# A two-layer graph transformer on one core: where the second layer's weight sums are kept at the border, and how many attention steps its first block takes

## The chip, the core and the metric

The kernel runs on one core of one Trainium2 chip. The metric is the time of one execution on the device in microseconds (us). Five engines work side by side: PE (TensorE: matmuls; PEld are its weight loads), DVE (VectorE), ACT (ScalarE), POOL (GpSimd) and SP (SyncE). Each runs its own instructions in order, and an instruction waits until what it needs has arrived. SP, ACT and POOL also issue the DMA transfers.

## The reference, cut to what matters

Two layers of the same form, with 2708 nodes, 512 features, 8 heads of 64 and a hidden width of 2048, all in float32. The adjacency is sparse, so a node attends to few others.

```python
def layer(h, adj, Wq, bq, Wk, bk, Wv, bv, Wo, bo, W1, b1, W2, b2, ln1_g, ln1_b, ln2_g, ln2_b):
    mask = adj.astype(float32) + eye(n)
    q, k, v = ((h @ W.T + b).reshape(n, 8, 64) for W, b in ((Wq, bq), (Wk, bk), (Wv, bv)))
    scores = einsum('nhd,mhd->hnm', q, k) / sqrt(64)
    attn = softmax(where(mask == 0, -1e9, scores))
    ctx = einsum('hnm,mhd->nhd', attn, v).reshape(n, 512)
    h1 = layer_norm(h + ctx @ Wo.T + bo, ln1_g, ln1_b)
    ff = relu(h1 @ W1.T + b1) @ W2.T + b2
    return layer_norm(h1 + ff, ln2_g, ln2_b)
x = layer(x, adj, *layer_0); x = layer(x, adj, *layer_1)
```

## The kernel before, in words

**Tiles and blocks.** The nodes are sorted by their number of neighbours and cut into 22 tiles of 128 (the last one, tile 21, has 20 rows). `CAPS` gives the longest list of neighbours in each tile. Two tiles make a block; a layer has 11 blocks, and the last is tiles 21 and 0. The code of `by_edges` issues everything in an order written out by hand.

**Attention** (`attend`, L1898 on) works on DVE, ACT and POOL. A step takes up to two neighbours per node: POOL gathers their keys and values (L1119, tile `kv`), DVE multiplies by the query (L1156) and sums per head (L1162), ACT takes the exponential (L1175) and weighs one neighbour's values (L1182), DVE weighs the other's (L1188) and adds (L1195). The weighing of a step is issued one step later. At a tile's end come a few small operations (L1203 to L1218) and the division on ACT (L1226), which gives `cx`. `loads` (L1249) issues the gathers three chunks ahead (`EARLY`). The `kv` tiles come from a ring of `KVB` = 5 places; in layer 1 `rows_of_keys` (L1233) adds the places of the weights `wk` and `wv`, which are free by then: seven in all, from its first gather on.

**Feed-forward** works on PE. A block has 16 chunks f of the hidden width: a product with W1 (tile `pf`), relu on ACT (`ft`), and a product with W2 into the accumulators `a0`, `a1`, three chunks later (`LAG`). In the blocks after `FORMED[n]` (1 in layer 0, 3 in layer 1), up to the last but one, `feed_forward_by_seven` (L1727) does the second product for pairs of chunks with seven matmuls in place of eight. It needs sums of the hidden values (L1735 to L1738, on DVE) and, for pairs 0 to 6, sums of blocks of W2, which are read back from `form_d` in HBM (L1720).

**How steps and blocks interleave.** At each chunk f of a block the loop calls `advance(x)`: x comes from tables (`PACES` for block 0, `PACE` for the blocks without the seven products, `PACE7` for those with them) and is added to a credit, which the next attention steps use up (a step of two neighbours costs 1, and no step starts with three `cx` waiting). At f = 10 and 11 `until` issues the steps that the next block's two tiles still need; then `attended` does the output projection, the residual and the first norm (its total is L1307). At the end of a block in layer 1 DVE takes the accumulators with another L1307; the rest of that norm follows in the next block (`ended`: squares on ACT, L1324; L1331 and L1333 on POOL; L1334 on DVE; scaling on ACT).

**The border of the layers.** In layer 0's last block (which has no seven products) SP loads layer 1's W1 and W2 as their places come free: pair j of W2 at f = 2j + 3. `form_apart` (L1677) makes layer 1's sums for pair j: four subtractions on DVE (L1684 to L1687) into the tile `forms`, and four stores of 128 KB to `form_d` (L1690). Pairs 0 to 4 are made at f = 7, 9, 11, 13 and 15 and stored from POOL's queue; pairs 5 and 6 follow the last keys and values and are stored from SP's. `staged` (L1669) takes three of the five `kv` places for `forms`; pair 6 uses the first of them a second time. `settle` (L1388) turns layer 1's short vectors at f = 13. When the block's chunks are done, DVE adds the accumulators of tile 21 to the residual (L1642, with three more additions at L636 since its 20 rows are summed in quarters, L1583), norms it (L1275 to L1290, L1281 on POOL), and PE transposes it (L1349) for layer 1's keys and values. Two queries of layer 1 from preloaded tiles (`zTs`) stand on PE around that transposition. Then `keys_values` finishes, its rows are put into `kv_d` (L1082), and layer 1 begins: some twenty queries on PE, with the first attention steps between them, and then its block 0.

**Use of the sums.** Layer 1 reads the fourth sum of each pair at block 3 (`form_in`, L1692), the other three from block 4 on.

Of the kernel before, what the change touches and what calls it, by code (L numbers as in the profile page):

```python
# [8 lines left out]
F32 = mybir.dt.float32  # L9
# [9 lines left out]
P = 128  # L19
DM = 512  # L20
# [3 lines left out]
NC = DM // P  # L24
# [13 lines left out]
SLOTS = 2  # L38
QB = 3
LAG = 3  # L40
KVB = 5
# [8 lines left out]
EARLY = 3  # L50
PACES = (
    (0.0,) * 4 + (0.85,) * 8 + (0.0,) * 2 + (0.8,) * 2,
    (0.75,) * 11 + (0.0,) * 2 + (0.9,) * 3,
)
PACE7 = (
    (0.0,) * 4 + (0.6,) + (1.3,) * 4 + (0.6,) * 2 + (0.0,) * 2 + (0.5, 0.8, 2.4),
# [431 lines left out]
def by_edges(ctx: ExitStack, tc: tile.TileContext, x, xT, adj, layers, out, redo):  # L488
# [9 lines left out]
    nc = tc.nc  # L498
# [16 lines left out]
    wts = ctx.enter_context(tc.tile_pool(name="wts", bufs=1))  # L515
# [4 lines left out]
    stage = ctx.enter_context(ExitStack())  # L520
# [15 lines left out]
    at = None  # L536
# [694 lines left out]
    places = []  # L1231
    written = [[] for _ in range(NL)]

    def rows_of_keys(n):

        if n == NL - 1 and not places:
            places.extend([None] * KVB + ["wk", "wv"])
        tag = places[0] if places else None
        if places:
            places.append(places.pop(0))  # L1240
        if tag is None:
            return at.tile([P, SLOTS, 2 * DM], F32, tag="kv", name="kv", bufs=KVB)
        kv = wts.tile([P, NC, DM], F32, tag=tag, name="kv")
        return kv.rearrange("p c n -> p (c n)").rearrange("p (s n) -> p s n", s=SLOTS)
# [113 lines left out]
    class Layer:  # L1358
        def __init__(self, n, w):
            self.n, self.w, self.w1, self.w2, self.due = n, w, [], [], None  # L1360
            self.apart, self.other = True, False
            self.stores = nc.sync

# [304 lines left out]

        def staged(self):  # L1669

            slots = []
            for _ in range(3):
                place = at.tile([P, SLOTS, 2 * DM], F32, tag="kv", name="forms", bufs=KVB)
                place = place.rearrange("p s n -> p (s n)")
                slots += [place[:, i * 2 * P : (i + 1) * 2 * P] for i in range(8)]
            return slots

        def form_apart(self, j, slots):
# [3 lines left out]
            i = 4 * j % len(slots)  # L1682
            t2, t3, t4, t1 = slots[i : i + 4]
            nc.vector.tensor_tensor(t3, b22, b12, ALU.subtract)  # L1684
# [333 lines left out]
    for n in range(NL):  # L2018
        last = n == NL - 1
        nxt = None if last else Layer(n + 1, layers[n + 1])  # L2020
        if n > 0:
            streamed = now.queries(order[10:16])
            got = {}
            ahead = attend(n, got)
            for _ in range(2):
                now.query(*pool.pop(0))
            next(ahead)
            both = now.two(order[8:10])
            pool += [(g, both[:, i]) for i, g in enumerate(order[8:10])]
# [36 lines left out]
        for k, block in enumerate(blocks):  # L2066
# [14 lines left out]
            for f, zs in enumerate(working):  # L2081
# [64 lines left out]
                if not last and not more:  # L2146
# [20 lines left out]
        if not last:  # L2167
# [69 lines left out]
```

## Time and profile before

| | us |
|---|---|
| median of 3 runs | 1830.86 (1828.04 to 1831.38) |
| the profiled execution's own time | 1829.8 |
| its span, first to last instruction | 1828.1 |
| PE busy | 1793.9 |
| DVE busy | 1463.7 |
| ACT busy | 1002.0 |
| POOL busy | 875.7 |

The stages of the span, from windows with PE's busy time in each: layer 0's keys, values and neighbour lists 0 to 150 (148.4), its queries 150 to 315 (163.2), its blocks to 1004 (682.1 of 689.0), its last block to 1064 (54.1 of 60.0), layer 1's queries to 1149.7 (85.4 of 85.7), its blocks 0 to 3 to 1409.8 (259.9 of 260.2), blocks 4 to 9 to 1782.3 (366.2 of 372.5), the last block and the end to 1828.1 (34.7 of 45.8).

How to read it: an engine is busy while it works on an instruction, and idle before one that waits; the trace names the instruction that ended the wait. The mean granted clock of PE is 0.994 of full speed.

### The profile page before, as it was taken

What the parts mean: (1) busy time and instruction counts of PE and PEld (TensorE: products, weight loads), DVE (VectorE), ACT (ScalarE), POOL (GpSimd) and SP (SyncE); (2) the same over time, 40 slices, a digit from 0 to 9 for tenths busy, and PEclk for the clock granted to TensorE, in tenths of its full rate; (3) what the DMA queues carried; (4) which work ended last, traced back from release to release, by engine and by line L of the source; (5) the groups of instructions that cost most, each with busy time, mean ns of one, the idle gap of its engine ahead of it and who ended that gap; (6) DMA issues with size and microseconds to landing.
All of it is one profiled execution on the core that took longest, in us unless ns stands there. A gap on an engine that the chain in (4) does not pass through costs nothing.

```text
span 1828.1 us, 23929 instructions
## 1 busy us (share of the span) xinstructions
PE 1793.9 (98%) x6839; PEld 1216.1 (67%) x6839; DVE 1463.7 (80%) x2599; ACT 1002.0 (55%) x3397; POOL 875.7 (48%) x847
## 2 busy tenths in 40 slices
PE   9999999999999999999999989999999999999987
PEld 4444455666777867778677534666666788788866
DVE  4986768987989889899895257968877899999943
ACT  5770435645556555564543204576766677677741
POOL 3334755534455544554430232546665765575412
PEclk9999999999999999999999999999999999999999
DMA  9997987756576676665652877946757887877621
GB/s 340 371 347 253 364 279 248 233 171 232 199 253 225 201 235 196 219 234 183 227 191 71 287 282 269 326 138 232 249 174 244 285 257 226 283 268 221 212 77 36
DMA packets 186296, 426.74 MB, mean 233 GB/s; under 512 B 20886, under 2 KB 83210, under 8 KB 186152
## 3 DMA queue, kind: packets, MB, share of 16 engines
q0 software_dynamic: 77520, 265.54, 43.8%
q1 hardware_dynamic: 98474, 137.96, 22.2%
q10 hardware_dynamic: 10158, 21.61, 3.1%
q8 instruction: 56, 0.92, 0.2%
q14 instruction: 88, 0.72, 0.1%
HBM read 357.13 MB, written 57.11 MB: 227 GB/s over the span
## 4 chain that ended last, share of the span: by engine, by line
PE 83%; DVE 8%; issue 4%; DMA 2%; ACT 2%; POOL 1%; POOLq 0%; DVEq 0%; SPq 0%; ACTq 0%
PE pf L1769 17%; PE c L1758 8%; PE k L626 8%; PE q L626 8%; PE v L626 8%; PE pf L1595 8%; PE o L626 7%; PE a L1568 7%; PE a L1758 6%; PE tp L1349 2%; DVE sc L1162 2%; DVE kv L1156 2%; PE a L1793 1%; PE a L1789 1%; DVE acc L1195 1%
## 5 line engine op out<-in xcount | busy, mean ns | idle before, releaser
L1119 POOL DMA_INDIRECT kv<-kv_d,listed x420 | 540.4, 1287 | 287.6 <-DVE acc L1195 129.8
L1769 PE MATMUL pf<-hT,w 128*128 128x256 f32 x1792 | 407.1, 379 | 1.6 <-ACT ft L1780 1.6
L1769 PEld LDWEIGHTS pf<-hT,w 128*128 128x128 f32 x1792 | 339.3, 190 | 58.3 <-issue 11.2
L1182 ACT ACTIVATE kv<-kv,p 128x64 f32<-128x64 f32 x1232 | 311.2, 336 | 5.0
L1156 DVE TENSOR_TENSOR kv<-kv,q 128x1024 f32<-128x1024 f32 (+1 forms) x222 | 257.1, 1158 | 11.2 <-DMA q<-q_d,ident_i 9.7
L1162 DVE TENSOR_REDUCE sc<-kv 128x16 f32<-128x1024 f32 (+1 forms) x222 | 258.0, 1162 | 7.6
L1195 DVE TENSOR_TENSOR acc<-acc,kv 128x1024 f32<-128x1024 f32 (+2 forms) x178 | 205.6, 1155 | 51.2 <-ACT kv L1182 37.3
L1595 PEld LDWEIGHTS pf<-hT,w 128*128 128x128 f32 x1024 | 178.4, 190 | 56.5 <-issue 33.5
L1595 PE MATMUL pf<-hT,w 128*128 128x256 f32 (+1 forms) x1024 | 214.7, 358 | 1.0 <-ACT ft L1606 0.9
L1780 ACT ACTIVATE ft<-pf,b 128x256 f32<-128x256 f32 x168 | 78.3, 468 | 214.7 <-PE pf L1769 212.1
L1568 PE MATMUL a<-w,ft 128*128 128x512 f32 x416 | 194.6, 592 | 0.0
L1175 ACT ACTIVATE p<-sc,listed 128x8 f32<-128x8 f32 x420 | 103.9, 296 | 129.6 <-DVE sc L1162 98.2
L1281 POOL TENSOR_TENSOR rd<-va,mhalf 128x1 f32<-128x1 f32 (+1 forms) x48 | 43.6, 908 | 234.6 <-DVE va L1279 234.5
L626 PE MATMUL o<-wo,cT 128*128 128x512 f32 x336 | 151.2, 594 | 2.3 <-issue 1.9
L1188 DVE TENSOR_TENSOR kv<-kv,p 128x512 f32<-128x512 f32 (+1 forms) x178 | 124.1, 697 | 6.3 <-ACT p L1175 6.1
L1568 PEld LDWEIGHTS a<-w,ft 128*128 128x128 f32 x416 | 77.7, 190 | 57.5 <-issue 52.3
L1331 POOL TENSOR_SCALAR va<-sq 128x1 f32<-128x1 f32 (+1 forms) x40 | 17.6, 441 | 197.5 <-ACT xb L1324 95.9
L626 PEld LDWEIGHTS o<-wo,cT 128*128 128x128 f32 x336 | 63.3, 190 | 72.0 <-issue 63.5
L751 DVE MAX8 tops<-code 128x8 f32<-128x247 f32 (+2 forms) x242 | 78.6, 400 | 27.2 <-ACT code L746 27.2
L1226 ACT ACTIVATE cx<-acc,su 128x64 f32<-128x64 f32 (+1 forms) x352 | 88.3, 334 | 14.1 <-DVE su L1218 9.0
L1606 ACT ACTIVATE ft<-pf,b 128x256 f32<-128x256 f32 (+1 forms) x112 | 50.4, 453 | 73.3 <-PE pf L1595 65.3
L1182 ACT ACTIVATE acc<-kv,p 128x64 f32<-128x64 f32 (+1 forms) x352 | 88.9, 335 | 1.4
(258 smaller groups left out, 2828.3 us busy)
## 6 DMA issues: line engine op xcount, KB each, us to landing
forms<-form_d SPq DMA_DIRECT2D x294, 128.0 KB
aj<-in_adj SPq DMA_DIRECT2D x42, 677.0 KB
kv_d<-kvs ACTq DMA_DIRECT2D x21, 512.0 KB
h<-ln_b POOLq DMA_DIRECT2D x41, 256.0 KB
xg<-in_xT SPq DMA_DIRECT2D x19, 512.0 KB
w<-in_W SPq DMA_DIRECT2D x16, 512.0 KB
kv<-kv_d,listed POOLq DMA_INDIRECT x420
zT_d<-zT SPq DMA_DIRECT2D x22, 256.0 KB
```

The lines of the kernel that those rows point to most:

```text
L626: nc.tensor.matmul(o[:r], xs(c), wm[:, c, :], start=(c == 0), stop=(c == NC - 1))
L1119: return nc.gpsimd.indirect_dma_start(out=to, out_offset=None, in_=table[:, :], in_offset=bass.IndirectOffsetOnAxis(ap=s, axis=0), bounds_ ...
L1156: nc.vector.tensor_tensor(kv[:r, :c, :DM], kv[:r, :c, :DM], self.q[:r].unsqueeze(1).to_broadcast([r, c, DM]), ALU.mult,)
L1162: nc.vector.tensor_reduce(self.sc[:r, s0 : s0 + c, :], kv[:r, :c, :DM].rearrange("p s (h d) -> p s h d", d=DK), AX.X, ALU.add,)
L1175: nc.scalar.activation(p[:r, s, :], self.sc[:r, s, :], AF.Exp, bias=minus[:r, g, s : s + 1])
L1182: nc.scalar.activation(to[:, i, hd], kv[:r, i, DM + h * DK : DM + (h + 1) * DK], AF.Copy, scale=p[:r, s0 + i, h : h + 1],)
L1188: nc.vector.tensor_tensor(to[:, 0, :].rearrange("p (h d) -> p h d", d=DK), kv[:r, 0, DM:].rearrange("p (h d) -> p h d", d=DK), p[:r, s0, : ...
L1195: nc.vector.tensor_tensor(self.acc[:r, :c, :], self.acc[:r, :c, :], kv[:r, :c, DM:], ALU.add)
L1568: nc.tensor.matmul(a[:r, cols], fts[f][:, c0 : c0 + r], self.w2[f // 2][:, f % 2, cols], start=(f == 0), stop=(f == NFC - 1),)
L1595: nc.tensor.matmul(pf[:, :w], self.w1[f // 2][:, c, f % 2 * P : f % 2 * P + P], hT[:, c, :w], start=(c == 0), stop=(c == NC - 1),)
L1758: nc.tensor.matmul(to, left, right, start=start, stop=stop)
L1769: nc.tensor.matmul(pf[:, :W], self.w1[j][:, c, f % 2 * P : f % 2 * P + P], hT[:, c, :], start=(c == 0), stop=(c == NC - 1),)
```

## The change

Three things change; no operation on data is added or dropped.

- **Places and order of the sums.** `staged` takes two `kv` places in the last block (pairs 0, 1 and 2), and, after the last keys and values, the places of `wk` (pairs 3 and 4) and `wv` (pairs 5 and 6). Pairs 0, 1, 2 are made at f = 9, 12, 15 of layer 0's last block; pairs 3 and 4 where 5 and 6 were; pairs 5 and 6 after layer 1's next two queries.
- **Stores.** A pair is stored by one transfer of 512 KB: pairs 0 to 2 from POOL's queue right after they are made, pairs 3 to 6 from SP's queue at f = 3 to 6 of layer 1's block 0. Until f = 7 of that block attention has five `kv` places; then `wk` and `wv` join, as before.
- **Pace.** Layer 1's row of `PACES` gives 0.95 in place of 0.75 for f = 0 to 10 and 1.1 in place of 0.9 for f = 13 to 15: 13.75 in place of 10.95 for block 0.

```diff
 PACES = (
     (0.0,) * 4 + (0.85,) * 8 + (0.0,) * 2 + (0.8,) * 2,
-    (0.75,) * 11 + (0.0,) * 2 + (0.9,) * 3,
+    (0.95,) * 11 + (0.0,) * 2 + (1.1,) * 3,
 )
@@ rows_of_keys
-            places.extend([None] * KVB + ["wk", "wv"])
+            places.extend([None] * KVB)
@@ Layer
-        def staged(self):
-            slots = []
-            for _ in range(3):
-                place = at.tile([P, SLOTS, 2 * DM], F32, tag="kv", name="forms", bufs=KVB)
-                place = place.rearrange("p s n -> p (s n)")
-                slots += [place[:, i * 2 * P : (i + 1) * 2 * P] for i in range(8)]
-            return slots
+        def staged(self):
+            if not self.stages:
+                for _ in range(2):
+                    self.stages.append(
+                        at.tile([P, SLOTS, 2 * DM], F32, tag="kv", name="forms", bufs=KVB)
+                    )
+                return
+            for i, tag in enumerate(("wk", "wv")):
+                place = wts.tile([P, NC, DM], F32, tag=tag, name="forms")
+                self.stages.append(place.rearrange("p (s a) n -> p s (a n)", s=SLOTS))
+
+        def stage(self, j):
+            place = self.stages[j // 2 if j < 3 else (j + 1) // 2]
+            place = place.rearrange("p s (i w) -> p (s i) w", w=2 * P)
+            a = 4 * (j % 2 if j < 3 else (j + 1) % 2)
+            return place[:, a : a + 4]
@@ form_apart
-            for i, t in enumerate((t2, t3, t4, t1)):
-                by = nc.gpsimd if j < 5 else nc.sync
-                by.dma_start(out=form_d[self.n][j, i], in_=t)
+
+        def form_out(self, j, by):
+            to = form_d[self.n][j].rearrange("i p w -> p i w")
+            by.dma_start(out=to, in_=self.stage(j))
@@ layer 1's start
-            for _ in range(2):
+            for j in (5, 6):
                 now.query(*pool.pop(0))
+                now.form_apart(j)
@@ the loop over a block's chunks
+                if n > 0 and k == 0 and 2 < f < 7:
+                    now.form_out(f, nc.sync)
+                if n > 0 and (k, f) == (0, 7):
+                    places.extend(["wk", "wv"])
...
-                        staged = nxt.staged()
-                    if f > 6 and f % 2:
-                        nxt.form_apart((f - 7) // 2, staged)
+                        nxt.staged()
+                    if f in (9, 12, 15):
+                        nxt.form_apart(f // 3 - 3)
+                        nxt.form_out(f // 3 - 3, nc.gpsimd)
@@ after layer 0's last block
-            for j in (5, 6):
-                nxt.form_apart(j, staged)
+            nxt.staged()
+            for j in (3, 4):
+                nxt.form_apart(j)
```

Three places show how rows move. First, DVE in layer 0's last block, from f = 13 to the first addition of tile 21 (L1642). Before (`w2_8260` is pair 3 of layer 1's W2, `w2_8292` pair 4; L1397 and L1392 are `settle`):

```order
L1684 TENSOR_TENSOR forms_8182<-w2_8260 128x256
L1685 TENSOR_TENSOR forms_8182<-w2_8260 128x256
L1686 TENSOR_TENSOR forms_8182<-w2_8260,forms_8182 128x256
L1687 TENSOR_TENSOR forms_8182<-w2_8260,forms_8182 128x256
L1397 TENSOR_SCALAR bv_8172<-pr_8330 128x4
L1397 TENSOR_SCALAR ln1_b_8174<-pr_8333 128x4
L1392 TENSOR_TENSOR ln1_b_8177<-ln1_b_8177,temp_8179 128x512
L1684 TENSOR_TENSOR forms_8183<-w2_8292 128x256
L1685 TENSOR_TENSOR forms_8183<-w2_8292 128x256
L1686 TENSOR_TENSOR forms_8183<-w2_8292,forms_8183 128x256
L1687 TENSOR_TENSOR forms_8183<-w2_8292,forms_8183 128x256
L1642 TENSOR_TENSOR h_7868<-a0_8089,h_7868 20x512
```

Now (the changed file's lines are some ten further down: L1694 is L1684, L1643 is L1642; `w2_8139` is pair 1, `w2_8211` pair 2):

```order
L1694 TENSOR_TENSOR forms_8181<-w2_8139 128x256
L1695 TENSOR_TENSOR forms_8181<-w2_8139 128x256
L1696 TENSOR_TENSOR forms_8181<-w2_8139,forms_8181 128x256
L1697 TENSOR_TENSOR forms_8181<-w2_8139,forms_8181 128x256
L1398 TENSOR_SCALAR bv_8172<-pr_8307 128x4
L1398 TENSOR_SCALAR ln1_b_8174<-pr_8310 128x4
L1393 TENSOR_TENSOR ln1_b_8177<-ln1_b_8177,temp_8179 128x512
L1694 TENSOR_TENSOR forms_8182<-w2_8211 128x256
L1695 TENSOR_TENSOR forms_8182<-w2_8211 128x256
L1696 TENSOR_TENSOR forms_8182<-w2_8211,forms_8182 128x256
L1697 TENSOR_TENSOR forms_8182<-w2_8211,forms_8182 128x256
L1643 TENSOR_TENSOR h_7868<-a0_8089,h_7868 20x512
```

Pairs 3 and 4 no longer stand ahead of tile 21's addition; pairs 0 to 2 do.

Second, DVE in layer 1's block 9: the last attention steps (each L1156 opens one) among the sums of hidden values. Before, the last but one and the last step:

```order
L1156 TENSOR_TENSOR kv_13924<-kv_13924,q_13471 128x2x512
L1162 TENSOR_REDUCE sc_13621<-kv_13924 128x16
L1188 TENSOR_TENSOR kv_13903<-kv_13903,p_13622 128x512
L1195 TENSOR_TENSOR acc_13687<-acc_13687,kv_13903 128x1024
L1735 TENSOR_TENSOR forms_10523<-ft_14122,ft_14095 128x128
L1736 TENSOR_TENSOR ft_14095<-ft_14095 128x128
L1737 TENSOR_TENSOR forms_10523<-forms_10523,ft_14095 128x128
L1738 TENSOR_TENSOR forms_10523<-ft_14122,forms_10523 128x128
L1156 TENSOR_TENSOR kv_14056<-kv_14056,q_13471 128x2x512
L1162 TENSOR_REDUCE sc_13621<-kv_14056 128x16
L1188 TENSOR_TENSOR kv_13924<-kv_13924,p_13622 128x512
L1195 TENSOR_TENSOR acc_13687<-acc_13687,kv_13924 128x1024
```

Now, at the place where the first of four steps stood (L1746 to L1749 are L1735 to L1738):

```order
L1156 TENSOR_TENSOR kv_13899<-kv_13899,q_13314 128x2x512
L1162 TENSOR_REDUCE sc_13535<-kv_13899 128x16
L1188 TENSOR_TENSOR kv_13838<-kv_13838,p_13536 128x512
L1195 TENSOR_TENSOR acc_13592<-acc_13592,kv_13838 128x1024
L1746 TENSOR_TENSOR forms_10587<-forms_10587 128x128
L1747 TENSOR_TENSOR forms_10587<-forms_10587 128x128
L1748 TENSOR_TENSOR forms_10587<-forms_10587 128x128
L1749 TENSOR_TENSOR forms_10587<-forms_10587 128x128
L1188 TENSOR_TENSOR kv_13899<-kv_13899,p_13536 128x512
L1195 TENSOR_TENSOR acc_13592<-acc_13592,kv_13899 128x1024
L1203 TENSOR_TENSOR acc_13592<-acc_13592 128x512
L1207 TENSOR_REDUCE peak_8486<-sc_13535 128x1
```

Block 9 has one step left where it had four; the tile's end (L1203) follows it at once.

Third, SP's transfers in layer 1's block 0 (`w_8920` is the last pair of W2, `q` a tile of queries that attention will use, `form_d_118` the sums in HBM). Now, with the stores (before, eight stores of 128x256 stood at the border, ahead of layer 1's third store of queries):

```order
L1387 DMA w_8920<-in_W 128x2x512
L1116 DMA q<-q_d_114 128x512
L581 DMA ln_g<-in_ln_g 128x512
L581 DMA ln_b<-in_ln_b 128x512
L1701 DMA form_d_118<-forms 128x4x256 x3
L1116 DMA q<-q_d_114 128x512
L1701 DMA form_d_118<-forms 128x4x256
L1479 DMA q_d_114<-qs 20x512
```

Four stores of 512 KB now stand in SP's queue in block 0, three of them ahead of a load of queries.

More of the change, by code (lines that the diff above doesn't have):

```diff
@@ L1360, in __init__ @@
             self.n, self.w, self.w1, self.w2, self.due = n, w, [], [], None
+            self.stages = []
             self.apart, self.other = True, False
@@ L1669, in staged, with form_apart @@
         def staged(self):
-            slots = []
-            for _ in range(3):
-                place = at.tile([P, SLOTS, 2 * DM], F32, tag="kv", name="forms", bufs=KVB)
-                place = place.rearrange("p s n -> p (s n)")
-                slots += [place[:, i * 2 * P : (i + 1) * 2 * P] for i in range(8)]
-            return slots
-        def form_apart(self, j, slots):
+            if not self.stages:
[12 more added lines that the diff above has]
+            return place[:, a : a + 4]
+        def form_apart(self, j):
             w, W = self.w2[j], 2 * P
             b11, b12, b21, b22 = w[:, 0, :W], w[:, 0, W:], w[:, 1, :W], w[:, 1, W:]
-            i = 4 * j % len(slots)
-            t2, t3, t4, t1 = slots[i : i + 4]
+            place = self.stage(j)
+            t2, t3, t4, t1 = (place[:, i] for i in range(4))
             nc.vector.tensor_tensor(t3, b22, b12, ALU.subtract)
```

## The prediction

> **What bounds the kernel now.** I read the page first, then the list of what PE waits for, then windows around PE's longest waits, then the timelines at those places. The busy line of the page and PE's waits (engine, line, what it waited for: us in total, times, longest):
>
> ```profile
> PE 1793.9 (98%) x6839; PEld 1216.1 (67%) x6839; DVE 1463.7 (80%) x2599; ACT 1002.0 (55%) x3397; POOL 875.7 (48%) x847
> PE tp L1349 <- DVE h L1290: 8.4, 4, 5.9
> PE tp L1349 <- ACT cx L1226: 5.0, 1, 5.0
> PE o L621 <- ACT cT L1354: 2.4, 1, 2.4
> ```
>
> PE is busy for 1793.9 of the span's 1828.1 us, and the change neither adds nor removes a matmul. All that it can win is idle time of PE and time at a lowered clock. Two single waits matter: 5.9 us for a norm on DVE, 5.0 us for a context (cx) that attention delivers. Windows around these two and around the 2.4 us wait (window, its length, PE, PEld, DVE, ACT and POOL busy, granted clock, DMA share, GB/s):
>
> ```profile
> 973.00:975.40 2.40, 0.01 (x1) 0.00 (x0) 1.02 (x5) 2.40 (x11) 0.00 (x0) 1.00 0.00 0
> 975.40:977.00 1.60, 1.58 (x9) 0.60 (x10) 0.02 (x1) 0.82 (x4) 0.00 (x0) 1.00 0.00 0
> ...
> 1057.40:1063.20 5.80, 0.00 (x0) 0.00 (x0) 5.12 (x10) 0.00 (x0) 3.03 (x5) 0.73 1.03 384
> 1063.20:1066.00 2.80, 2.73 (x7) 1.65 (x8) 2.40 (x6) 0.00 (x0) 0.78 (x1) 0.50 0.02 6
> 1066.00:1070.00 4.00, 4.00 (x15) 1.10 (x14) 2.04 (x3) 0.78 (x4) 0.62 (x2) 0.88 0.19 66
> ...
> 1747.60:1752.60 5.00, 0.01 (x1) 0.01 (x1) 4.69 (x10) 0.99 (x5) 0.00 (x0) 0.70 0.00 0
> 1752.60:1755.00 2.40, 2.39 (x6) 1.42 (x7) 2.29 (x6) 2.19 (x9) 0.00 (x0) 0.50 0.00 0
> 1755.00:1757.00 2.00, 2.00 (x7) 1.59 (x7) 0.15 (x1) 1.35 (x5) 0.48 (x2) 0.64 0.22 65
> ```
>
> After 2.4 us of idleness the clock stayed at 1.00; after 5.8 and 5.0 us it was at 0.50. What that costs: 2.80 x 0.50 + 4.00 x 0.12 = 1.9 us at the border, 2.40 x 0.50 + 2.00 x 0.36 = 1.9 us near the end. A wait that goes takes its slow stretch along.
>
> **The border of the layers.** DVE's timeline, then PE's (start, us, engine line, operation; in brackets the idle time before it and its releaser):
>
> ```profile
> 1040.65 0.42 DVE L1684 TENSOR_TENSOR forms<-w 128x256 f32<-128x256 f32 x1 [6.51 <-DMA w<-in_W]
> ...
> 1052.94 0.43 DVE L1684 TENSOR_TENSOR forms<-w 128x256 f32<-128x256 f32 x1 [10.61 <-DMA w<-in_W]
> ...
> 1055.82 0.42 DVE L1684 TENSOR_TENSOR forms<-w 128x256 f32<-128x256 f32 x1 [0.46 <-DMA w<-in_W]
> ...
> 1057.42 0.67 DVE L1642 TENSOR_TENSOR h<-a,h 20x512 f32<-20x512 f32 x1
> ```
> ```profile
> 1050.96 1.05 PE L1583 MATMUL a<-w,ft 128*20 128x512 f32 x8
> ...
> 1053.77 3.60 PE L626 MATMUL q<-wq,zTs 128*128 128x512 f32 x8
> ...
> 1063.27 0.61 PE L1349 MATMUL tp<-ident,h 20*128 20x20 f32 x4 [5.91 <-DVE h L1290]
> ```
>
> The 20-row tile's sum is complete on PE at 1050.96 + 1.05 = 1052.0. DVE takes it up only at 1057.42, since the sums of pairs 3 and 4 stand ahead of it and wait for their halves of W2 (landed at 1052.94 and 1055.82). From there to PE's transposition is 1063.27 - 1057.42 = 5.9 us of DVE and POOL work. In the new order pairs 0, 1 and 2 alone stand ahead; the third pair of weights had landed by 1040.65, and pair 2 now comes two steps after settle, at about 1047. So DVE is free at 1052.0, the transposition can start at 1052.0 + 5.9 = 1057.9, and PE's query ends at 1053.77 + 3.60 = 1057.4. Of 5.9 us of idleness 0.5 us stay, and below the 2.4 us of the row above no clock is lost: 5.4 + 1.9 = 7.3 us. I take off 0.3 us, because the zT of the 20-row tile also waits for POOL's memset, which follows the next tile's norm: -7.0 us. The keys, values, puts and gathers of the next layer hang on PE's last matmuls there, so they come as much earlier and attention keeps its distance to PE.
>
> The Trainium skill (TensorE: Matmul & The Clock Gate, Part 1) states that an idle window of about 3.4 us halves the clock until about 3.4 us of busy time have passed. Worked out from that page, an estimate, each drop costs 1.7 us instead of 1.9, and the whole sum would be 0.4 us smaller. The trace agrees with it: 0.50 after both long waits, 1.00 after the short one.
>
> **Where the moved work goes.** Pairs 3 and 4 take the place on DVE that 5 and 6 had behind the last keys. Pairs 5 and 6, 8 operations of 0.42 us, follow the next two evictions of queries, where DVE was idle:
>
> ```profile
> 1085.90 0.69 DVE L1467 SCALAR_TENSOR_TENSOR qs<-q,bq 128x512 f32<-128x512 f32 x1 [2.74 <-PE q L626]
> ```
>
> 1.7 us a pair fit in 2.7 us of waiting; uncovered they would delay the next eviction by less than that, and PE has more than one psum tile for queries. Stores: POOL issues 3 instead of 20, SP none at the border instead of 8 (which frees the q_d store and the zT loads behind them), and 4 of 512 KB in block 0. Those 2 MB stand in SP's queue ahead of a load of q and of the residuals, which are wanted three or more steps later; with the rate below they take 5 us. PE doesn't wait for any of this: 0 us. If the load of q came late, its cost would be at most these 5 us.
>
> **The attention steps.** A step takes one row here per L1156. Counting these rows against the ends of the blocks in both orders, 20, 31, 43, 55 steps stand ahead of the ends of blocks 0 to 3 before, 22, 34, 47, 59 now; then three more than before up to block 8 (110 for 107), so that block 9 has one step to do instead of four. What it had (DVE), and what PE waited for:
>
> ```profile
> 1726.81 1.22 DVE L1156 TENSOR_TENSOR kv<-kv,q 128x1024 f32<-128x1024 f32 x1
> ...
> 1751.71 0.20 DVE L1218 RECIPROCAL su<-su 128x8 f32<-128x8 f32 x1
> ```
> ```profile
> 1746.53 1.05 PE L621 MATMUL o<-wo,cT 128*20 128x512 f32 x8
> ...
> 1752.59 1.91 PE L1349 MATMUL tp<-ident,cx 128*128 128x128 f32 x4 [5.00 <-ACT cx L1226]
> ```
>
> Its first step began at 1726.81 and now is the last. Three steps fewer at the pitch below are 13.1 us: the reciprocal comes at 1751.7 - 13.1 = 1738.6, with cx some 2 us later well ahead of 1747.6. What is late next there is PE itself. Gain: 5.0 + 1.9 = 6.9 us.
>
> Who pays: blocks 0 to 2. Windows of blocks 0, 1 and 2 and block 0's DVE timeline:
>
> ```profile
> 1149.65:1217.98 68.33, 68.33 (x241) 42.70 (x241) 53.70 (x68) 42.29 (x156) 31.23 (x29) 1.00 0.68 238
> 1217.98:1281.69 63.71, 63.71 (x225) 41.12 (x225) 51.34 (x73) 44.28 (x161) 38.23 (x34) 1.00 0.69 222
> 1281.69:1345.51 63.82, 63.82 (x226) 41.05 (x225) 51.90 (x67) 45.65 (x167) 40.03 (x36) 1.00 0.67 214
> ```
> ```profile
> 1191.07 1.23 DVE L1195 TENSOR_TENSOR acc<-acc,kv 128x1024 f32<-128x1024 f32 x1 [0.82 <-ACT kv L1182]
> 1194.34 0.69 DVE L1307 CUSTOM_DVE_ANT_0 h<-o,xb 128x512 f32<-128x512 f32 x1 [2.05 <-PE o L626]
> ...
> 1201.66 0.69 DVE L1307 CUSTOM_DVE_ANT_0 h<-o,xb 128x512 f32<-128x512 f32 x1 [6.43 <-PE o L626]
> ...
> 1204.10 1.22 DVE L1156 TENSOR_TENSOR kv<-kv,q 128x1024 f32<-128x1024 f32 x1
> ...
> 1208.47 1.21 DVE L1156 TENSOR_TENSOR kv<-kv,q 128x1024 f32<-128x1024 f32 x1
> ```
>
> Pitch: 1208.47 - 1204.10 = 4.37 us. Block 0 gets two steps ahead of its first L1307: 8.7 us against 2.05 + 6.43 = 8.5 us of idleness. DVE is late by 0.3 us at the second L1307 and on time, nearly, at the block's end. DVE goes from 53.7 to 62.4 of 68.3 us there, and to about 55.7 and 56.3 of 63.8 in blocks 1 and 2. Block 2's extra step stands behind L1307, so its end comes some 3.3 us late on DVE (the steps there include one of half size), and block 3 ends the same way. What follows a block's end, shown at block 4's start (DVE, ACT, PE):
>
> ```profile
> 1412.25 0.15 DVE L1318 TENSOR_SCALAR nm<-zsum 128x1 f32<-128x1 f32 x1
> ```
> ```profile
> 1413.70 0.68 ACT L1324 ACTIVATE a<-h,nm 128x512 f32<-128x512 f32 x1
> ...
> 1415.11 0.46 ACT L1780 ACTIVATE ft<-pf,b 128x256 f32<-128x256 f32 x1
> ```
> ```profile
> 1409.67 10.52 PE L1769 MATMUL pf<-hT,w 128*128 128x256 f32 x48
> ```
>
> ACT's squares have 1.3 us to spare; 3.3 us more hold the relu behind them back by 2.0 us, to 1417.1. PE's fifth chunk, which needs that psum place, begins at 1409.67 + 4 x 10.52 / 6 = 1416.7, so a wait of about 0.9 us. For a block with three such places it is nothing. Bounds for all new waits in blocks 0 to 4: 0 and 3.3 us; I take 0.7, near what the rows give.
>
> **The sum.** 1829.8 us is the profiled execution's own time; its span is 1828.1, with 1.7 around it. -7.0 - 6.9 + 0.7 = -13.2, so 1816.6 us. The three runs' median is 1830.9, 1.1 above the profiled one: 1817.7 against it. I predict **1817.5**. 0.2% is 3.7 us, about what a measurement here can tell from no change.
>
> **The rivals.**
> *Gathers starve (slower).* Until chunk f = 7 of block 0 attention has five kv places instead of seven: the gather for step m+3 waits for the sum of step m-2. Rows of POOL's waits, of the first chunk's second gather and its use, and of that time's transfers:
>
> ```profile
> POOL kv L1119 <- DVE acc L1195: 129.8, 45, 9.2
> ```
> ```profile
> 1086.01 1.01 POOL L1119 DMA_INDIRECT kv<-kv_d,listed  x1 [0.30 <-issue]
> ```
> ```profile
> 1094.13 1.23 DVE L1156 TENSOR_TENSOR kv<-kv,q 128x1024 f32<-128x1024 f32 x1 [0.67 <-issue]
> ```
> ```profile
> 1100.00:1120.00 20.00, 20.00 (x48) 8.69 (x47) 17.71 (x25) 9.26 (x37) 6.32 (x6) 1.00 1.04 413
> ```
>
> Three steps, 13.1 us, lie between the release and the use; two issues of 1.3 us and a landing of L must fit. At a share of 1.04 L was 1094.1 - 1087.0 = 7 us: 9.7 in all. A step's pitch becomes (2.6 + L) / 3 once L passes 10.5 us. At L = 18 it is 6.9: 2.5 us more on 13 steps, 33 us, of which DVE's 8.5 us of idleness take a part, so PE waits 24 us and the time is 1817.5 + 24 = 1842. The sign turns at 13.2 + 8.5 = 21.7 us over 13 steps, L = 15.5. For it: the four stores fall in the same stretch. Against it: layer 0 runs on five places with PE full. Chance 0.07 (with other new waits that eat it all).
> The Trainium skill (DMA: Bandwidth & Descriptors, Queues, rings and completion order) states that each DMA engine takes turns between the queues that have work. By it the stores of SP's queue at most halve the gathers' rate while they last, 5 us, so L goes to some 12; no run here shows it yet.
> *The border stays.* If something else, settle's rows or a late pair, keeps DVE from 1052.0, its 7.0 us are not won: 1824.5. The loads were issued ahead of those that had landed by 1040.65, which speaks against it. 0.10.
> *The end stays.* If DVE's lag through blocks 4 to 8 grows and cx is late all the same, its 6.9 us stay: 1824.4. Against it: as many steps a block as before, and three fewer in block 9. 0.07.
> *Nothing to see.* Both give way to new waits, within 3.7 us of 1830.9. 0.04.
>
> **How the numbers follow.** Both waits go: 0.72, at 1814.5 (no new wait, and 1.7 us of the runs' own spread and smaller waits) to 1820.1 (3.3 us of new waits). With the two cases of one wait, 0.17, the range reaches 1824.5, and 0.11 is left out above. Faster: 0.72 + 0.17 = 0.89; I keep 0.01 of it for same. Same 0.05, slower 0.07.
>
> **What would show it.** In the profile of the changed kernel: L1290's wait on PE at the border under 1 us and the clock there 1.00; no wait for cx in block 9; DVE near 62 of 68 us in block 0, with PE still full; POOL waiting for acc in block 0 without DVE waiting for kv. Wrong: DVE waiting for kv or q in block 0, PE waiting at the starts of blocks 1 to 4 for over 3.3 us in sum, or the old waits with other releasers.

## The result, and the profile after

The changed kernel takes **1817.56 us** (median of 4 runs, 1817.08 to 1819.66), the kernel before 1830.70 (4 runs beside it, 1828.04 to 1831.38): a ratio of 0.9933, 95% interval 0.9916 to 0.995. Run again later, beside other kernels, the change took 1817.26 us (5 runs), at the same 0.9933. One later execution of the kernel before took 2716 us and stands in no ratio. The change is 0.7% faster, as forecast; where the time went differs from the forecast, most of all in one term, which the prediction put at nothing.

The changed kernel's page and its list of what PE waits for (us in total, times, longest):

```profile
span 1815.1 us, 23887 instructions
PE 1791.5 (99%) x6839; PEld 1214.6 (67%) x6839; DVE 1463.3 (81%) x2599; ACT 1001.1 (55%) x3397; POOL 855.4 (47%) x830
```
```profile
PE tp L1349 <- DVE h L1290: 3.1, 4, 1.0
PE o L621 <- ACT cT L1354: 2.4, 1, 2.4
PE pf L1780 <- ACT ft L1791: 2.1, 4, 0.8
PE q L626 <- DVE acc L1195: 1.6, 1, 1.6
...
PE q L626 <- DMA zT<-zT_d: 0.5, 1, 0.5
```

The 5.9 us for the norm and the 5.0 us for cx are gone from the list. Two new rows stand there: PE waits 1.6 and 0.5 us for queries (q, L626). The first is put down to DVE's acc, which the query does not use. It was a transfer too: the trace's semaphore events have the last part of its zT landing at 1117.69, and the query starts at 1117.82.

**The border.** DVE's timeline, then PE's, at the 20-row tile:

```profile
1050.73 0.68 DVE L1643 TENSOR_TENSOR h<-a,h 20x512 f32<-20x512 f32 x1 [3.49 <-PE a L1584]
...
1055.80 0.74 DVE L1290 SCALAR_TENSOR_TENSOR h<-h,rd,ln_b 20x512 f32<-20x512 f32 x1 [0.47 <-POOL rd L1281]
```
```profile
1052.36 3.60 PE L626 MATMUL q<-wq,zTs 128*128 128x512 f32 x8
1056.59 0.42 PE L1349 MATMUL tp<-ident,h 20*128 20x20 f32 x4 [0.63 <-DVE h L1290]
...
1067.20 1.02 PE L626 MATMUL v<-wv,zT 128*128 128x512 f32 x2
```

DVE now waits for PE's sum, not the other way round: it takes it up at 1050.73, and of 5.9 us of PE's idleness 0.63 are left.

**The end.** PE in block 9:

```profile
1697.86 1.99 PE L1780 MATMUL pf<-hT,w 128*128 128x256 f32 x8 [0.34 <-ACT ft L1791]
1700.23 1.32 PE L1349 MATMUL tp<-ident,h 128*128 128x128 f32 x8 [0.38 <-ACT h L1340]
...
1741.30 1.05 PE L621 MATMUL o<-wo,cT 128*20 128x512 f32 x8
1742.29 0.66 PE L1349 MATMUL tp<-ident,cx 128*128 128x128 f32 x4
1747.53 3.60 PE L626 MATMUL o<-wo,cT 128*128 128x512 f32 x8
```

From the 20-row tile's o to the turned cx there are 0.99 us, where the kernel before took 6.06, and the transposition takes 0.66 us instead of 1.91: the clock is not lowered. Two small waits, where PE turns to block 9, are new.

**Where the time went.** The same work of PE set side by side in the two traces; how far the changed kernel is ahead there, and what the stretch up to it gave. Two of its rows rest on waits of the kernel before that were not shown yet, in its layer 0 and in layer 1's block 8 (PE):

```profile
440.84 3.70 PE L626 MATMUL o<-wo,cT 128*128 128x512 f32 x8 [1.07 <-issue]
...
1685.38 3.70 PE L626 MATMUL o<-wo,cT 128*128 128x512 f32 x8 [0.88 <-issue]
```

| work of PE | before | changed | ahead | the stretch gave |
|---|---|---|---|---|
| first query at the border | 1053.77 | 1052.36 | 1.4 | 1.4: unchanged code in layer 0, the stall of 1.07 us did not come again |
| v of the border's last tile | 1075.40 | 1067.20 | 8.2 | **6.8**: the wait at the border |
| block 0's first pf | 1149.48 | 1143.69 | 5.8 | **-2.4**: layer 1's queries |
| block 9's first o | 1694.11 | 1687.45 | 6.7 | 0.9: the wait of 0.88 us in block 8 |
| the 20-row tile's o | 1746.53 | 1741.30 | 5.2 | **-1.4**: block 9's start |
| the last o | 1760.11 | 1747.53 | 12.6 | **7.4**: the wait for cx |
| the span's end | 1828.1 | 1815.1 | 13.0 | 0.4 |

The two waits are put down to "issue" alike, but they are not alike. The one of 1.07 us comes in none of the ten other traces that have the same code there: the 1.4 us of the first row are this execution's, not the change's. The one of 0.88 us is also in the two later traces with the old row of paces (0.87 us in border_only and in five_places, both below), and in no trace with a new one. The line of border_only:

```profile
1677.51 3.70 PE L626 MATMUL o<-wo,cT 128*128 128x512 f32 x8 [0.87 <-ACT cT L1354]
```

So it is a wait for a context, like the one in block 9, and its 0.9 us are a gain of the change that nobody forecast. The loss of 1.4 us at block 9's start belongs to the change as well, as it is 1.4 in pace_only too. That makes 13.0 - 1.4 = 11.6 us for the change between these two executions; the medians differ by 13.1 us.

**The queries.** Where the 2.4 us went: PE's queries, SP's loads of zT and POOL's gathers in the changed kernel.

```profile
1098.10 13.90 PE L626 MATMUL q<-wq,zT 128*128 128x512 f32 x32
1112.54 3.67 PE L626 MATMUL q<-wq,zT 128*128 128x512 f32 x8 [0.55 <-DMA zT<-zT_d]
1117.82 3.67 PE L626 MATMUL q<-wq,zT 128*128 128x512 f32 x8 [1.61 <-DVE acc L1195]
```
```profile
1101.73 3.75 SPq L1454 DMA_DIRECT2D zT<-zT_d  x2
...
1108.59 0.32 SPq L1454 DMA_DIRECT2D zT<-zT_d  x1
```
```profile
1086.71 0.99 POOL L1119 DMA_INDIRECT kv<-kv_d,listed  x1 [0.30 <-issue]
1094.24 1.32 POOL L1119 DMA_INDIRECT kv<-kv_d,listed  x1 [6.55 <-DVE qs L1468]
...
1108.48 0.99 POOL L1119 DMA_INDIRECT kv<-kv_d,listed  x1 [0.30 <-issue]
```

The last zT of these queries is asked for at 1108.59, when its buffer comes free, and is used at 1117.82: 9.2 us for 256 KB, of which the transfer takes 9.1. Before, the same load took 4.0 us to land (1116.79 to 1120.82, by the semaphore events) and PE did not wait. POOL's gathers stop at 1087.7 for 6.55 us, since all five kv places are taken (nine gathers fill them, as one step here has a single neighbour), and the last of them go out as late as 1108.48, into the time of that load. Windows of both kernels, set at the same distance from the border's last v (GB/s is the last column; the changed kernel first):

```profile
1096.00:1108.00 12.00, 12.00 (x30) 5.30 (x29) 11.28 (x17) 4.60 (x19) 5.70 (x6) 1.00 0.95 315
1108.00:1116.00 8.00, 7.45 (x18) 2.93 (x16) 6.75 (x8) 4.29 (x19) 1.16 (x2) 1.00 1.03 406
```
```profile
1104.20:1116.20 12.00, 12.00 (x30) 5.28 (x28) 10.01 (x15) 4.54 (x19) 3.03 (x3) 1.00 1.03 415
1116.20:1124.20 8.00, 8.00 (x20) 3.41 (x19) 6.76 (x8) 4.24 (x19) 0.00 (x0) 1.00 0.66 252
```

Before, the transfers ran at some 410 GB/s until the backlog was done, and slackened (252) when the last zT was loaded. In the changed kernel they lose 100 GB/s over 12 us to the gap, and are full when that load needs them.

### The profile page after: what moved, and what is told of

Read it like the earlier page. It is cut to its first block, busy times and chain, and to the rows that moved or that the text cites. A ratio compares the mean times of both kernels' runs of the same rounds, so it can differ in the third digit from the quotient of the medians.

```text
span 1815.1 us, 23887 instructions
## 1 busy us (share of the span) xinstructions
PE 1791.5 (99%) x6839; PEld 1214.6 (67%) x6839; DVE 1463.3 (81%) x2599; ACT 1001.1 (55%) x3397; POOL 855.4 (47%) x830
## 5 line engine op out<-in xcount | busy, mean ns | idle before, releaser
L1119 POOL DMA_INDIRECT kv<-kv_d,listed x420 | 526.0, 1252 | 307.2 <-DVE acc L1195 145.8
L1156 DVE TENSOR_TENSOR kv<-kv,q 128x1024 f32<-128x1024 f32 (+1 forms) x222 | 257.1, 1158 | 14.1 <-DMA q<-q_d,ident_i 10.9
L626 PE MATMUL o<-wo,cT 128*128 128x512 f32 x336 | 151.0, 593 | 0.3 <-ACT cT L1354 0.3
L626 PEld LDWEIGHTS o<-wo,cT 128*128 128x128 f32 x336 | 63.4, 190 | 69.3 <-issue 59.6
L746 ACT ACTIVATE code<-aj 128x1354 bf16<-128x1354 int32 (+1 forms) x44 | 73.5, 1724 | 23.7 <-POOL aj L740 19.0
```

What stands on the lines that cost most here:

```text
L626: nc.tensor.matmul(o[:r], xs(c), wm[:, c, :], start=(c == 0), stop=(c == NC - 1))
L1119: return nc.gpsimd.indirect_dma_start(out=to, out_offset=None, in_=table[:, :], in_offset=bass.IndirectOffsetOnAxis(ap=s, axis=0), bounds_ ...
L1156: nc.vector.tensor_tensor(kv[:r, :c, :DM], kv[:r, :c, :DM], self.q[:r].unsqueeze(1).to_broadcast([r, c, DM]), ALU.mult,)
```

## The experiments

The theory after the result: the two gains are separate, each from its own edit, and the loss in the queries comes from five places instead of seven. Rivals: the gains share a cause; the loss comes from the moved sums on DVE or from the bytes on the queues. Each ratio below is against the kernel before on the same chip.

**The two edits, each by itself.** Only the table's row, on the kernel before:

```diff
-    (0.75,) * 11 + (0.0,) * 2 + (0.9,) * 3,
+    (0.95,) * 11 + (0.0,) * 2 + (1.1,) * 3,
```

> The kernel before with the new pace alone. Theory (two separate gains, one loss): PE's 5.0 us wait for cx in block 9 goes with its slow clock, nothing else changes, so 6 to 7 us faster: 1824 us, with the 5.9 us wait at the border still there. Rival (the gain is the border's alone, and steps taken earlier cost PE as much in blocks 0 to 4): within 2 us of the kernel before, 1830.7.

And the changed kernel with that row undone:

```diff
-    (0.95,) * 11 + (0.0,) * 2 + (1.1,) * 3,
+    (0.75,) * 11 + (0.0,) * 2 + (0.9,) * 3,
```

> The changed kernel with the old pace. Theory: the border wins 6.8 us (its wait and slow clock), five kv places until f = 7 of block 0 lose 2.4 us in layer 1's queries, and the wait for cx in block 9 stays at 4 to 6 us: 4.4 us faster, 1826.3. Rival (the 2.4 us in the queries come from something else that moved by itself): 6.8 us faster, 1823.9, no PE wait of over 0.5 us between the border and block 0.

Measured: 1824.01 us, ratio 0.9962 (0.9948 to 0.9975), and 1825.01 us, 0.9972 (0.996 to 0.9983), beside 1831.01. PE's waits, the paces alone first, then the border alone:

```profile
PE tp L1349 <- DVE h L1290: 8.4, 4, 5.9
```
```profile
PE tp L1349 <- ACT cx L1226: 5.0, 1, 5.0
PE tp L1349 <- DVE h L1290: 3.1, 4, 1.0
...
PE q L626 <- DMA zT<-zT_d: 0.9, 1, 0.9
```

Each edit takes its own wait away and leaves the other's. 7.0 + 6.0 = 13.0 us, against the whole change's 13.1 by its first runs and 14.4 by its later ones (each beside its own kernel before): within the spread of the runs, some 1 to 2 us, they add. The paces alone give the 6.9 us that were forecast for the end; the border alone falls 1 us short of its 7.0, and has a new wait in the queries. Counted from the border's last v, block 0 begins 0.95 us later there than before, where the two traces of the change lose 2.4 and 2.2: the code up to block 0 is the same, so the size of this loss varies from execution to execution.

**Five places alone.** The kernel before, whose wk and wv become kv places as late as in the change:

```diff
-            places.extend([None] * KVB + ["wk", "wv"])
+            places.extend([None] * KVB)
...
+                if n > 0 and (k, f) == (0, 7):
+                    places.extend(["wk", "wv"])
```

> The kernel before, in which wk and wv join the kv places only at f = 7 of block 0; nothing else differs. Theory (the gathers of the sixth chunk on wait for a place, run 4 to 6 us later and collide with the loads of zT for PE's queries): PE waits 1.5 to 3 us between the border and block 0, and the time is 1832 to 1834. Rival (pairs 5 and 6 on DVE between the queries, or the moved stores, make that loss): no such wait, 1830.7.

Measured: 1833.10 us, ratio 1.0012 (1.0003 to 1.0021; 11 runs): 2.1 us slower than 1831.01. Its list has the end's wait as before (and the border's, 5.8 us), and the change's new one:

```profile
PE tp L1349 <- ACT cx L1226: 5.0, 1, 5.0
...
PE q L626 <- DMA zT<-zT_d: 1.4, 2, 1.1
```

So late places cost about the 2 us, with no sum moved; the last zT takes 8.4 us to land (1117.57 to 1125.95).

**Seven places, all seven pairs stored at once.** The change's order of the sums, with pairs 0 to 2 in kv buffers and stored by POOL, pairs 3 to 6 stored by SP at the border, so that wk and wv are places from the first gather. The lines are against the changed kernel and cut: three kv places hold the sums again, as in the kernel before, and pairs 5 and 6 leave the queries:

```diff
-                if n > 0 and k == 0 and 2 < f < 7:
-                    now.form_out(f, nc.sync)
-                if n > 0 and (k, f) == (0, 7):
-                    places.extend(["wk", "wv"])
...
-            for j in (3, 4):
-                nxt.form_apart(j)
+            for j in (3, 4, 5, 6):
+                nxt.form_apart(j, staged)
```

> The new pace, and pairs 0, 1, 2 alone ahead of tile 21's norm as in the change; but three kv places hold the sums, pairs 3 to 6 are all made after the last keys and stored from SP's queue there, 2 MB, and attention has seven places from its first gather on. Theory: the border's and block 9's gains as in the changed kernel, and no PE wait in the queries: 2.2 us less than the change, 1815.4. Rival (sums on chip are needed, since 2 MB of stores at the border hold the first gathers and the queries' loads back): PE waits 2 to 5 us in the queries, 1817.5 to 1821.

Measured: 1818.36 us, ratio 0.9934 (0.992 to 0.9947). The 2 us are not won back. The first gather (POOL), the first step (DVE), and PE's wait:

```profile
1077.22 1.06 POOL L1119 DMA_INDIRECT kv<-kv_d,listed  x1 [4.34 <-issue]
```
```profile
1088.37 1.22 DVE L1156 TENSOR_TENSOR kv<-kv,q 128x1024 f32<-128x1024 f32 x1 [3.07 <-DMA kv<-kv_d,listed]
```
```profile
PE q L626 <- DMA zT<-zT_d: 1.7, 1, 1.7
```

Counted from the border's last v, the first gather goes out 1.0 us later than in the change and the first step starts 1.5 us later. With seven places PE waits 1.7 us for zT again, which takes 8.6 us to land: 2 MB of stores are 1 MB more than before the change, 2.5 us at the 413 GB/s of this trace from 1096 to 1108, and from 1108 to 1116 the transfers still run at 369 GB/s, where the kernel before had slackened to 252. The number of places by itself is therefore not the cause. What counts is when the backlog of transfers is done, beside the last load of zT.

**Six places.** The mean of the two: pairs 3 and 4 stored at the border (1 MB, as many bytes as the kernel before stored there), wk a place from the start, pairs 5 and 6 in wv as in the change:

```diff
-            places.extend([None] * KVB)
+            places.extend([None] * KVB + ["wk"])
...
-                if n > 0 and k == 0 and 2 < f < 7:
+                if n > 0 and k == 0 and 4 < f < 7:
...
-                    places.extend(["wk", "wv"])
+                    places.append("wv")
...
             for j in (3, 4):
                 nxt.form_apart(j)
+                nxt.form_out(j, nc.sync)
```

> The changed kernel, but pairs 3 and 4 are stored at the border (1 MB, as the kernel before stored there) and their place joins the kv places from layer 1's start: six places until f = 7 of block 0, where the seventh joins. Theory (places): the gathers' gap of 6.6 us in the changed kernel goes, the transfers are saturated without a break again and end earlier; PE's waits in the queries fall from 2.2 to under 1 us: 1816.0. Rival (bytes): 1 MB of stores at some 410 GB/s takes 2.4 us of the same transfers, about as much as the gap wasted, so the last zT load lands as late as now: 1817.5, PE waiting 1.5 to 2 us at the last streamed query.

> Six places once more, unaltered. Theory: its trace's 2.5 us are real, and the median of its first runs (1816.8) was drawn up by the runs' own spread of 2 us: 1815.2 us, ratio 0.9915. Rival: executions that are not profiled gain less, since the transfers land otherwise there: 1816.8 again, ratio 0.9922, which the runs can't tell from the change's 0.9933.

Measured: 1816.76 us (5 runs), ratio 0.9922 (0.9908 to 0.9935), and 1815.43 (4 runs), ratio 0.9912 (0.9896 to 0.9929). The transfers in the windows shown above, in the first of these traces:

```profile
1096.00:1108.00 12.00, 12.00 (x29) 5.33 (x28) 10.77 (x13) 3.52 (x15) 4.73 (x5) 1.00 1.03 412
1108.00:1116.00 8.00, 8.00 (x20) 3.61 (x19) 7.20 (x12) 4.89 (x22) 0.00 (x0) 1.00 0.73 280
```

POOL's gap shrinks from 6.55 to 3.25 us, the transfers keep 412 GB/s, where the change has 315, and the backlog is done in the last window (280, where the change has 406). The last zT lands in 5.5 us, and PE waits for no query. Taken from the border's last v, block 0 begins 2.6 and 2.5 us earlier in the two traces of this version than in the first of the change, and 2.5 and 2.3 us earlier than in the second; the nine runs' median is 1815.58 us against 1817.48 of the change's nine. The two intervals of the ratio overlap: that this version is faster in the queries is shown by the traces, and that it is faster as a whole is likely by the times.

**One query first.** The changed kernel with the query of order[16], whose zT comes through another buffer, ahead of the last streamed one:

```diff
-                if len(got) < 2 or i < 3:
+                if i < 5 and (len(got) < 2 or i < 3):
                     advance(0.65)
+                if i == 4:
+                    until(blocks[0][0])
+                    early[n] = now.attended(blocks[0], got, None, True)
+                    next(early[n])
+                    now.query(order[16], both[:, 0])
-            until(blocks[0][0])
-            early[n] = now.attended(blocks[0], got, None, True)
-            next(early[n])
-            now.query(order[16], both[:, 0])
             until(blocks[0][1])
```

> The changed kernel with one query (tile order[16], whose zT has landed) moved ahead of the last streamed query in layer 1's queries, with the first context's transposition; nothing else moves, and as many steps stand ahead of the blocks' ends. Theory: the changed kernel's loss there is the late landing of single zT loads (0.55 and 1.61 us of PE's waits), so 3.6 us of other work ahead of the last one takes its 1.6 us away: block 0 starts 1.6 us earlier, 1816.0 us against the changed kernel's 1817.6. Rival: the loss is the transfers' whole backlog, and the next thing to be late (the moved tile's own zT, issued at 1105.57, or the second context's cT) takes its place: 1817.6, with a wait of 1 to 2 us one query on.

Measured: 1817.62 us, ratio 0.9922 (0.9908 to 0.9936), beside a kernel before of 1831.62; the runs can't tell it from the change. PE:

```profile
1113.87 3.67 PE L626 MATMUL q<-wq,zT 128*128 128x512 f32 x8 [0.36 <-DMA zT<-zT_d]
```
```profile
1144.03 7.17 PE L1596 MATMUL pf<-hT,w 128*128 128x256 f32 x32 [0.70 <-ACT hT L1354]
```

The wait of 1.6 us goes, and half of it comes back ahead of block 0, where the moved query had covered the turning of h. Counted from the border's last v, block 0 begins 1.2 us earlier than in the change's first trace; as this stretch varies by itself, that is not shown to come from the edit.

**One step instead of two.** The kernel before with a row halfway:

```diff
-    (0.75,) * 11 + (0.0,) * 2 + (0.9,) * 3,
+    (0.85,) * 11 + (0.0,) * 2 + (1.0,) * 3,
```

> The kernel before with layer 1's row of paces 0.85 and 1.0, halfway to the change's: 21, 33, 45, 57 steps stand ahead of the ends of blocks 0 to 3, and 108 of 111 ahead of block 9 (107 before, 110 in the change). Theory: block 9's wait is a matter of steps at 4.4 us each, so one step fewer there leaves 5.0 - 4.4 = 0.6 us of wait, too short to lose the clock: 5.0 + 1.9 - 0.6 = 6.3 us, 1824.7 beside 1831.0. Rival: the wait hangs on something else than the number of steps (the order of sums and steps in block 9), and one step takes less than half: 1828 or above, with 2.5 us or more of waiting for cx.

Measured: 1831.69 us, ratio 1.0005 (0.9996 to 1.0014; 11 runs). Nothing is gained. PE in blocks 5, 7 and 9:

```profile
1462.62 1.38 PE L1349 MATMUL tp<-ident,h 128*128 128x128 f32 x8 [2.04 <-ACT h L1340]
...
1588.77 1.27 PE L1349 MATMUL tp<-ident,h 128*128 128x128 f32 x8 [1.41 <-ACT h L1340]
...
1755.36 1.52 PE L621 MATMUL o<-wo,cT 128*20 128x512 f32 x8 [2.48 <-ACT cT L1354]
```

At the end the wait is 2.5 instead of 5.0 us (the theory left 0.6) and now for another context, and the clock holds, so a step does count there, for about half of its 4.4 us. But the step stands elsewhere on the way: it delays the norms at the ends of two blocks, and PE waits for their h, 3.45 us in sum. After the first of these waits the granted clock is 0.50 from 1463.64 to 1467.05, another 1.7 us. What is gained at the end is spent there, near what the rival had. The number of steps ahead is not a dial; where each one falls decides.

**The same for layer 0.** Layer 0's block 9 has a wait of 2.4 us of the same kind. Two ways to have one step more ahead, each on the changed kernel, the second also on six places (six_late):

```diff
-    (0.0,) * 4 + (0.85,) * 8 + (0.0,) * 2 + (0.8,) * 2,
+    (0.0,) * 4 + (0.95,) * 8 + (0.0,) * 2 + (0.9,) * 2,
```

> The changed kernel with the same idea in layer 0: its block 0's row of paces 0.95 and 0.9 instead of 0.85 and 0.8, which puts one step more ahead of blocks 0 to 9. Theory: the wait of 2.4 us for cT in layer 0's block 9 goes like layer 1's wait for cx (a step is 4.4 us), without a clock to win back, since it was 1.00 there: 1815.2 us. Rival: layer 0's block 0 has no room on DVE, or gathers of five places don't keep up there, so PE waits by as much at the early blocks' ends: 1817.6 or above.

```diff
-    (0.0,) * 2 + (0.6,) * 3 + (1.2,) * 4 + (0.6,) * 2 + (0.0,) * 2 + (0.8,) * 3,
+    (0.0,) * 2 + (0.6,) * 3 + (1.2,) * 4 + (0.6,) * 2 + (0.0,) * 2 + (1.0,) * 3,
```

> The changed kernel with that step of layer 0 moved alone. Theory: what made layer 0's earlier start of the steps lose (4.2 us at block 0's end, with a wait of 3.1 us for cT and a clock of 0.70 behind it) was the place where the step stood, ahead of the contexts that the next block needs; at the end of block 1 it stands in DVE's idle time, so the 2.4 us go and nothing comes: 1815.2 us. Rival: the step makes the end of another block late by 1 to 4 us, as in the two runs with a step at another place: 1816.5 to 1819.

> Six places (the run before), and one attention step of layer 0 moved from block 9 to the end of block 1 (block 1's last three paces 1.0 instead of 0.8), where DVE waits 2.85 and 1.18 us for PE's o in the trace. Theory: both gains add: the queries' 2.2 us of PE's waits and the 2.4 us of the wait for cT in layer 0's block 9: 1817.6 - 2.2 - 2.4 = 1813.0 us. Rival: six places are worth less than their trace says (their median was 0.9 us below the changed kernel's) and the step only moves the wait: 1816 to 1817.5.

> The changed kernel once more, unaltered, beside the two below on the same chip: 1817.6 us by its first runs, within 1 us.

Measured: 1820.92 us, ratio 0.9942 (0.9929 to 0.9956); 1820.44, 0.9946 (0.9933 to 0.996); six_late 1819.95, 0.9935 (0.9921 to 0.9948); the change beside the last two 1817.26. All are some 3 to 4 us slower than what they start from. The first one's PE, then its clock there:

```profile
296.29 5.29 PE L626 MATMUL o<-wo,cT 128*128 128x512 f32 x8 [3.13 <-ACT cT L1354]
```
```profile
296.10:299.51 3.41, 3.22 (x4) 1.52 (x5) 3.10 (x4) 1.25 (x5) 1.88 (x2) 0.50 0.84 291
```

The second one's (layer0_late) PE, and its clock:

```profile
482.05 0.66 PE L1349 MATMUL tp<-ident,h 128*128 128x128 f32 x4 [0.85 <-DVE h L1290]
484.19 1.12 PE L1349 MATMUL tp<-ident,h 128*128 128x128 f32 x4 [1.48 <-DVE h L1290]
...
791.11 1.08 PE L1349 MATMUL tp<-ident,h 128*128 128x128 f32 x4 [1.48 <-DVE h L1290]
...
977.56 1.99 PE L1780 MATMUL pf<-hT,w 128*128 128x256 f32 x8 [1.43 <-ACT ft L1791]
```
```profile
483.98:487.40 3.42, 3.21 (x10) 2.77 (x11) 3.26 (x10) 1.14 (x4) 2.81 (x3) 0.50 0.41 116
791.18:794.59 3.41, 3.41 (x11) 2.88 (x12) 3.24 (x10) 1.14 (x4) 2.80 (x3) 0.50 0.53 148
```

The wait at layer 0's end shrinks from 2.4 to 1.4 us, and longer ones come on the way, in blocks 3 and 7 in the second, where PE turns what the block before has normed. Each of the two pairs of waits (0.85 and 1.48 us, 0.96 and 1.48) is followed by 3.41 us at half clock, up to 1.7 us each, so the two drops are up to 3.4 of the 5.0 us that this trace is behind the change's at the border. A step that fits DVE's idle time in the trace of one order pushes the next blocks' norms by some of its 4.4 us. In six_late the queries gain 2.0 us over layer0_late, by the two traces, near what six places gained over the change.

Sums kept on chip together with seven places were not tried.

## Why the prediction was right, and where not

- **The border, -7.0 us**: measured 6.8. 0.63 us of idleness stayed (0.5 forecast) and the clock held at its full value, since DVE was free when PE's sum came. That waits below 2.4 us cost no clock, as the prediction took from one row, is not so in general (see the last section); the 0.63 us are far below what any trace here shows to cost it.
- **"PE doesn't wait for any of this: 0 us"**, of the stores, the moved sums and the places: this step failed, by 2.4 us in this trace (2.2 in the second of the change, 0.95 in border_only's). The prediction looked at the places only for attention's sake, and there it was right: from 1075 to 1130 gathers took a median of 9.3 us to land, and from 1143 to 1175, with the four stores, 9.1, against the 15.5 at which that rival decides; in block 0 DVE never waited for kv.

```profile
kv<-kv_d,listed POOLq DMA_INDIRECT x17, 9.3
```

  What it did not ask is who else uses the transfers when the gathers go out later: the last loads of zT, on which PE hangs in layer 1's queries. Five places alone cost 2.1 us by the medians, more bytes at the border 1.9 by the trace, and six places with the old bytes nothing. The landing of the last zT tells them apart: 4.0 us before and 5.5 with six places, where PE did not wait; 7.7 (border_only), 8.4, 8.6 and 9.1 us where it did.
- **The attention steps, -6.9 us**: the end itself gave 7.4 us, and block 8 another 0.9, less 1.4 at block 9's start; the paces alone gave 7.0 by the medians. The reciprocal that ends the last context comes at 1731.73, some ten us ahead of PE's need.
- **New waits, +0.7 us in blocks 0 to 4**: none came there (0.3 us in all, as before). 0.7 us of new waits came at block 9's start, where 1.4 us were lost. DVE was busy for 60.92 of 67.36 us in block 0, near the 62.4 of 68.3 forecast, with PE at 67.06:

```profile
1143.69:1211.05 67.36, 67.06 (x238) 42.04 (x237) 60.92 (x78) 46.54 (x175) 39.26 (x34) 1.00 0.86 293
```

- **The sum**: forecast -13.2 from the profiled execution, measured 13.0. The agreement of these two traces is in part luck: the 2.4 us lost in the queries and the 0.7 us more than forecast at block 9's start were made up by 0.9 us in block 8, some 0.5 more than forecast at the end, and 1.4 us of stalls in layer 0 of before's execution, which are not the change's. By the traces the change is worth 11.6 us, by the medians 13.1; no run here settles the 1.5 us between, though one drop of the clock that some executions have and others not is worth as much (last section).
- **The rivals**: neither wait stayed, attention did not starve, and the two edits turned out to be independent, as the cases took them to be.

## What to carry to other kernels

When a change takes buffers from a prefetcher, ask not only whether its own user starves: the transfers that can no longer go early go later, and the one to check is whichever load has the least lookahead in that later stretch. Count bytes and buffers together, since giving the buffers back by storing more can cost as much. When work is moved ahead of a late wait, look at each block's end on the way: a step of 4.4 us at the wrong place costs as much as the wait it removes, so one step more may win nothing where two win 7 us. Before a stall is put down to chance, look for it at the same place in other traces: of two that looked alike here one was the change's.

## What the runs showed of the hardware

The clock fell after less idleness than the prediction's two examples show. In every trace of this case its changes, from the first rise on, lie a whole number of steps of 3.41 us apart (in layer0_late it is 0.50 from 483.98 to 487.40, as above, and again 90 steps later, from 791.18). What decides is how long PE was idle within one such step, not the length of a wait: all 16 drops ahead of PE's last matmul follow a step with 1.98 us or more of idleness, and no step with 1.86 us or less was followed by one. So two short waits in one step count as one, and a single wait of 2.4 us may fall whole into a step or be split between two. Layer 0's wait of 2.4 us, the same in eleven traces, left the clock at 1.00 in eight, the kernel before's and the change's among them, and in three it did not (pace_only, five_places, pace_one_step). The first of these, the step with the wait and the next one:

```profile
970.85:974.26 3.41, 1.30 (x7) 0.79 (x5) 2.24 (x10) 2.30 (x10) 0.00 (x0) 1.00 0.00 0
974.26:977.67 3.41, 3.12 (x12) 1.38 (x13) 0.68 (x1) 1.09 (x6) 0.00 (x0) 0.50 0.02 5
```

A drop of one step costs up to 3.41 x 0.50 = 1.7 us, so executions of one kernel can differ by that much. The Trainium skill (TensorE: Matmul & The Clock Gate, Part 1) states a window of about 3.4 us that runs freely, and half the clock after an idle window. The traces agree with the window; here a window a little over half idle was enough.

A store of 512 KB in one instruction kept POOL for 0.75 to 0.85 us, where the same bytes in four instructions had kept it for 2.2 to 2.3. In the windows of layer 1's queries above with a DMA share of 1.03 the transfers ran at 406 to 415 GB/s, so in such a stretch a megabyte (1024 KB) is some 2.5 us.
